# The first batch of a two-layer graph network: another order for its convolution

## The chip, the cores and the metric

The kernel runs on one core of one Trainium2 chip. The metric is the device time of one execution in microseconds (us). TensorE is called PE (its weight loads PEld), VectorE DVE, ScalarE ACT, GpSimd POOL and SyncE SP. Each engine works through its own queue in the order written; here that order is fixed by the program and not by a scheduler.

## The reference

There are 64 graphs of 256 nodes with 256 channels, all in float32. For this change, layer 0 matters:

```python
xc = transpose(x)                                    # channels first
h = relu(bn(conv1d(xc, conv1_w)))                    # "conv1": 1 tap
h = bn(conv1d(h, conv2_w, pad=8))                    # 17 taps along the nodes
x_conv = transpose(relu(h + xc))
s = x @ w_se.T + b_se                                # 3 numbers for each node
A = exp(-squared distances of s) * adj
msg = relu(x @ w_msg.T + b_msg)
x_nmp = A @ msg
# GRU gates: r, z = sigmoid(...), n = tanh(...) of [x_conv, x_nmp] and x
x = layernorm(x + (1 - z) * n + z * x)
# layer 1: layernorm, aggregation over adj, two projections, relu, layernorm
```

## The kernel before

The graphs go in eight batches of eight. The 17-tap convolution is not done tap by tap. The nodes of a graph are 16 positions (`j`) in 16 tiles (`t`); an exact polynomial transform over the positions (a tree of small rotations on DVE) turns the convolution into 16 "leaf" products with transformed filters on PE, three real products for each complex leaf. An inverse tree on DVE follows. The transformed filters have to be made once, in the first batch, from the weights; later batches read them back from DRAM (`w2m`).

In the main loop (one step for each graph) the gates and the second layer of a graph alternate on PE with pieces of the next batch's convolution; `pump()` hands out the pieces. Ahead of the loop the convolution of batch 0 has to be done alone, beside the making of the filters. That stretch is what the change touches:

```python
def filters(pool):            # 74 blocks of 7 output channels, in 20 groups of (mostly) 4
    ...                       # wt: 6 pieces of w2T, two buffers, fetched as buffers come free
    for i, (piece, starts) in enumerate(groups):
        WS[i + 2] = scaled(...)                    # DVE: ws = wt * scale of bn2
        TT[i + 1] = turned(WS[i + 1], ...)         # PE: 4 transposes; ACT: copy to tT
        for a, o in enumerate(starts):
            nc.tensor.matmul(ps, TT[i][:, a, :], tap_sb)      # PE: the taps' transform
            nc.scalar.copy(W2[0][:, c, :, ...], ps)           # ACT: into w2all
        # ... after the last group of an input half: six stores of w2all to w2m (6 MB)
        yield

def conv(b):
    # ... fetch(0), fetch(2): x of two graphs each
    yield None
    for g in range(0, BG, 2):                      # four pairs of graphs
        xTc = conv_pool.tile([P, C, 2 * N], F32, tag="xTc", bufs=1)
        # PE: 8 transposes of x; ACT: 2 copies into xTc; store of xTc to DRAM (xt); fetch(g + 4)
        for o in range(C):
            # PE: conv1, 2 matmuls of 512 columns
            # ACT: relu and batch norm into HP, 2 activations of 256
            yield PE_WEIGHT * 1.7
    yield None
    for j, r in ((0, 8), (8, 0)):                  # the fold: 4 operations of 2048 elements
        for first, op in ((V + r, ALU.subtract), (U + r, ALU.add)):
            nc.vector.tensor_tensor(...)
    yield from split_all(*TREES[0], S)             # DVE: the tree of V
    yield from butterflies([(S, V, V + 8, 8, True)])
    if b == 0: yield from split_u()                # DVE: the trees of U
    STAGE[b] = "products"
    # 8 items: products (PE), then take() (ACT copy, two DVE operations),
    # then merge steps (DVE), queued and handed out between the items
    STAGE[b] = "inverse"
    # second level: 8 operations of 512; third level: 8 operations of 512  (DVE)
    for q in range(4):
        xb = x_by_tiles(b, q)                      # 512 KB of x
        nc.vector.tensor_add(sl(V + 4 * q, 4), sl(V + 4 * q, 4), xb)
        # ... then 8 transposes (PE) and 4 relu activations (ACT) into xcs

# the first batch
fl = filters(first_pool)
# ... constants loaded: wms, rows, whh, wrr ...
for i in range(n_groups):                          # 20
    next(fl)
    while total < FRONT * (i + 1) / n_groups and 0 not in STAGE:
        total += next(first) or 0.0                # pieces of conv(0), conv1 among them
# ... conv(0) up to "inverse"; first_pool (w2all and the filters' buffers) closed
wih = weight(wihT, 2 * D, 3 * D, "wih", nc.sync, work)
for k in range(3):
    load(k)                                        # xT and adj of graph k
load_x(0)
early = [messages(0), messages(1), factors(0), distances(0), mask(0), factors(1),
         distances(1), mask(1), passing(0), messages(2)]
# ... one of them after every 1.5 units of conv(0)'s rest; then the main loop
```

`sl(a, n)` is `n` slots of the tile `XF`, 256 elements each; `stt` is DVE's scalar_tensor_tensor.

Of the kernel before, what the change touches and what calls it, by code (L numbers as in the profile page):

```python
# [12 lines left out]
F32 = mybir.dt.float32  # L13
# [3 lines left out]
P = 128  # L17
# [28 lines left out]
FRONT = 66.0  # L46
# [29 lines left out]
def gnn_two_layers(  # L76
# [38 lines left out]
    def x_by_tiles(b, q):  # L115

        t = conv_pool.tile([P, 4, D], F32, tag="xb", name="xb")
        nc.sync.dma_start(
            out=t, in_=x[b * BG:(b + 1) * BG].rearrange("g (t j) d -> (g t) j d", j=M)[:, 4 * q:4 * q + 4, :])
        return t  # L120
# [8 lines left out]
    tap_sb = const.tile([TAPS * OB, NM * OB], F32)  # L129
    nc.scalar.dma_start(out=tap_sb, in_=tb_dram.ap())  # L130
# [24 lines left out]
    def along_rows(pool):  # L155

        for i, v in enumerate((bn_scale[1], bn_shift[1])):
            ps = bank("ps_row")
            for c in range(C):
                dg = pool.tile([P, P], F32, tag="dg", name="dg", bufs=4)  # L160
                nc.vector.tensor_scalar(dg, ident, v[:, c:c + 1], None, ALU.mult)
                nc.tensor.matmul(ps[:, c * P:(c + 1) * P], ones, dg, start=True, stop=True)
            nc.scalar.copy(bn2_row[:, i, :], ps[:, :D])
# [3 lines left out]
    W2 = {}  # L167

    def filters(pool):
        W2[0] = pool.tile([P, C, NM, D], F32, name="w2all")  # L170
# [37 lines left out]
        along_rows(pool)  # L208
        TT = {}
        WS = {0: scaled(*groups[0]), 1: scaled(*groups[1])}  # L210
        TT[0] = turned(WS[0], 4)
        for i, (piece, starts) in enumerate(groups):
# [7 lines left out]
            for a, o in enumerate(starts):  # L220
                ps = bank("ps_w")
                nc.tensor.matmul(ps[:, :NM * OB], TT[i][:, a, :], tap_sb, start=True, stop=True)
                skip = OB - D % OB if o == D - OB else 0
                pv = ps[:, :NM * OB].rearrange("p (f o) -> p f o", o=OB)
                nc.scalar.copy(W2[0][:, c, :, o + skip:o + OB], pv[:, :, skip:])
            if i + 1 == len(groups) or pieces[groups[i + 1][0]][0] != c:
                for f in range(0, NM, 8):
                    g = min(f + 8, NM)
                    nc.sync.dma_start(out=w2m[f:g, c].rearrange("f p o -> p f o"), in_=W2[0][:, c, f:g, :])
# [60 lines left out]
    def merge(re, im, size, phis, scales, tmp, new):  # L290


        h, n = size // 2, len(phis)
        t_re, t_im = tmp, tmp + n * h
        same = all(abs(x0 - x1) < 1e-12 for s0, s1 in scales for x0, x1 in zip(s0, s1))
        for base, t in ((re, t_re), (im, t_im)):
            a, b = halves(base, n, size, False), halves(base, n, size, True)
            tt = temps(t, n, h)
            if same:
                nc.vector.tensor_sub(tt, a, b)  # L300
                yield cost(n * h)
                nc.vector.tensor_add(a, a, b)
                yield cost(n * h)
                continue

            assert n == 1 and h % 2 == 0
            for j in range(2):
                rho = scales[0][1][j] / scales[0][0][j]
                a2, b2 = sl(base + j, h // 2, 2), sl(base + h + j, h // 2, 2)
                stt(sl(t + j, h // 2, 2), b2, -rho, a2)  # L310
                yield cost(h // 2)
                stt(a2, b2, rho, a2)
                yield cost(h // 2)
        for k, phi in enumerate(phis):
            tan, c, turned = quarter(phi / 2)
            hr, hi = sl(re + k * size + h, h), sl(im + k * size + h, h)
            dr, di = sl(t_re + k * h, h), sl(t_im + k * h, h)
            if turned:
                stt(hr, dr, -tan, di)
                yield cost(h)  # L320
                stt(hi, di, -tan, dr, op1=ALU.subtract)
            else:
                stt(hr, di, tan, dr)
                yield cost(h)
                stt(hi, dr, -tan, di)
            yield cost(h)
            new.append(scales[k][0] + [c * s for s in scales[k][0]])
# [16 lines left out]
    def merges(which, p, tmp, scales):  # L344
# [4 lines left out]
        while True:  # L349
            below = ([1.0], [1.0]) if s == 2 else (scales[s // 2, 2 * n], scales[s // 2, 2 * n + 1])  # L350
            new = []
            yield from merge(re + n * s, im + n * s, s, [levels[-(s.bit_length() - 1)][n]], [below], tmp + n * s, new)
            scales[s, n] = new[0]
            if s == size or n % 2 == 0:
                return
            n, s = n // 2, 2 * s
# [65 lines left out]

    def conv(b):
# [14 lines left out]
        for g in range(0, BG, 2):  # L438
# [12 lines left out]
            for o in range(C):  # L451
# [7 lines left out]
                yield PE_WEIGHT * 1.7  # L459
        yield None  # L460
        for j, r in ((0, 8), (8, 0)):
            hv = HP[:, j:j + 8].rearrange("p j c g k -> p (j c g) k")
            for first, op in ((V + r, ALU.subtract), (U + r, ALU.add)):
                nc.vector.tensor_tensor(sl(first, 8).rearrange("p s (r t) -> p (s r) t", t=M),  # L464
                                        hv[:, :, 0:M], hv[:, :, 1:M + 1], op)
                yield cost(8)
# [9 lines left out]
        for _ in range(4):  # L476
            yield None
        sv, s8, s4 = {}, {}, {}
        todo = [(lambda k=k: products(b, 2 * k, S + 2 * k), merges(0, k, S, sv)) for k in range(4)]
        todo += [(lambda k=k: products(b, 8 + 2 * k, S2 + 2 * k), merges(1, k, S2, s8)) for k in range(2)]  # L480
        todo += [(lambda: products(b, 12, S2 + 4), merges(2, 0, S2 + 4, s4)), (lambda: last_products(b), None)]
        vector = deque([other])
        share, spent = (39.0 if b == 0 else 61.0) / len(todo), 0.0
        beyond = 1.0 - 0.85 * 5.2 / (share + 2 * cost(2))
        for i, (make, after) in enumerate(todo):
# [14 lines left out]
            if after:  # L500
# [12 lines left out]
        for j in range(4):  # L513
# [4 lines left out]
        for j in range(8):  # L518
            stt(sl(V + j, 2, 8), sl(V + j, 2, 8), sv[j], sl(U + j, 2, 8))
            yield cost(2)  # L520

        xcs = [work.tile([P, C, 4, N], F32, tag="xc", name="xc", bufs=3) for _ in range(2)]

# [13 lines left out]
        for q in range(4):  # L537
            xb = x_by_tiles(b, q)
# [9 lines left out]
        for g in range(BG):  # L548
            XC[b * BG + g] = (xcs[g // 4], g % 4)
# [4 lines left out]
    def load(k):  # L554
# [3 lines left out]
        XT[k] = work.tile([P, C, N], F32, tag="xT", name="xT", bufs=4)  # L558
        nc.sync.dma_start(out=XT[k], in_=xt_dram[k // 2][:, :, (k % 2) * N:(k % 2 + 1) * N])
        ADJ[k] = work.tile([P, C, N], F32, tag="adj", name="adj", bufs=5)  # L560
# [7 lines left out]
    def messages(k):  # L568
        MSG[k] = work.tile([P, C, D], F32, tag="msg", name="msg", bufs=3)
        st = sts[k % len(sts)]  # L570
        twice = st.rearrange("p m (r e) -> p m r e", e=SR)
        for m in range(C):
            ps = bank("ps_msg")
            for c in range(C):
                nc.tensor.matmul(ps[:, :D + 4], XT[k][:, c, m * P:(m + 1) * P], wms[:, c, :],  # L575
                                 start=(c == 0), stop=(c == C - 1))
            nc.vector.tensor_add(twice[:, m, :, 0:3], ps[:, D:D + 3].unsqueeze(1).to_broadcast([P, 2, 3]),
                                 bse_row.unsqueeze(1).to_broadcast([P, 2, 3]))
            nc.vector.tensor_add(MSG[k][:, m, :], ps[:, :D], bmsg)  # L579
        nc.scalar.activation(MSG[k], MSG[k], AF.Relu)  # L580

        sq = work.tile([P, C, 3], F32, tag="sq", name="sq")
        ns = work.tile([P, C], F32, tag="ns", name="ns", bufs=3)
# [7 lines left out]
    def factors(k):  # L591
# [4 lines left out]
        lr = work.tile([ROWS, 2, N], F32, tag="lr", name="lr", bufs=1)  # L596
# [4 lines left out]
    def distances(k):  # L601
        lr, ns = ST[k]
        AT[k] = work.tile([P, C, N], F32, tag="AT", name="AT")
# [146 lines left out]
    first, total = conv(0), 0.0  # L750
    with tc.tile_pool(name="first", bufs=1) as first_pool:
        fl = filters(first_pool)
# [3 lines left out]


# [15 lines left out]
        bse_row = const.tile([P, 3], F32)  # L773
        nc.sync.dma_start(out=bse_row, in_=bse.rearrange("r o -> o r").to_broadcast([P, 3]))
        bmsg = const.tile([P, D], F32)
        nc.sync.dma_start(out=bmsg, in_=rows[:, R_MSG:R_MSG + D].to_broadcast([P, D]))
# [6 lines left out]
        bhh = first_pool.tile([P, 2 * D], F32, name="bhh")  # L783
        nc.sync.dma_start(out=bhh, in_=rows[:, R_HH:R_HH + 2 * D].to_broadcast([P, 2 * D]))
# [8 lines left out]
        total += next(first)  # L793
        n_groups = 20
        for i in range(n_groups):
            next(fl)
            while total < FRONT * (i + 1) / n_groups and 0 not in STAGE:
                total += next(first) or 0.0
        for _ in fl:
            pass  # L800
        nc.vector.tensor_add(brzn[:, :2 * D], brzn[:, :2 * D], bhh)
        nc.gpsimd.tensor_scalar(wrr, wrr, 0.5, None, ALU.mult)
        nc.gpsimd.tensor_scalar(brel, brel, 0.5, None, ALU.mult)
        while STAGE.get(0) != "inverse":
            total += next(first) or 0.0

    work = ctx.enter_context(tc.tile_pool(name="work", bufs=2))
    wih = weight(wihT, 2 * D, 3 * D, "wih", nc.sync, work)
    for k in range(3):
        load(k)  # L810
    load_x(0)
    early = [lambda: messages(0), lambda: messages(1), lambda: factors(0), lambda: distances(0), lambda: mask(0),
# [118 lines left out]
```

## Time and profile before

The time is the median of three runs; the rest is from the profile of one execution, whose span is 2314.6 us.

| | |
|---|---|
| median (lowest to highest) | 2314.66 us (2311.76 to 2317.57) |
| PE busy | 2225.2 us (96%) |
| DVE busy | 1685.2 us (73%) |
| ACT busy | 766.0 us (33%) |
| POOL busy | 468.7 us (20%) |
| mean DMA rate | 98 GB/s |

A line of the timeline shows start and length in us, engine, line, operation, output and inputs with their shapes, count, and in brackets how long the engine had been idle and what ended that. The table by stages shows a window, its length and the busy time and instruction count of each engine. A float32 matmul is two records on PE, a transpose one. Busy time of PE is modelled, since matmuls are pipelined; a stage with PE always busy can still be one at a low clock, so the granted clock stands beside it.

### The profile page before, as it was taken

The numbers are of one execution on the slowest core, as the hardware profiler recorded it, in microseconds if no ns is written. First come the engines' busy times: TensorE is split into PE (matmuls) and PEld (weight loads), VectorE is DVE, ScalarE is ACT, GpSimd is POOL, SyncE is SP. The second block draws the span as 40 slices with busy tenths as digits, with TensorE's granted clock in tenths as the row PEclk, the third lists the DMA queues.
The fourth block names the chain that finished last, engine by engine and source line by source line (L and its number), as shares of the span: only waits on it lengthen the run. The fifth ranks groups of instructions, "written<-read, shape, count | busy, mean of one in ns | idle before, by whom it ended". The sixth has DMA issues, their size and how long they took to land.

```text
span 2314.6 us, 24215 instructions
## 1 busy us (share of the span) xinstructions
PE 2225.2 (96%) x8262; PEld 1456.2 (63%) x8262; DVE 1685.2 (73%) x3212; ACT 766.0 (33%) x1577; POOL 468.7 (20%) x925
## 2 busy tenths in 40 slices
PE   7879999999999999999999999999999999999996
PEld 4565566666666666666666566665666656666663
DVE  2893998759794788829887498956889398874543
ACT  4514222442224321353224332253223532243332
POOL 1000221312122222202212131221222122121211
PEclk8998999999999999999999999999999999999998
DMA  5543152224323144221532234222433214321100
GB/s 176 156 161 114 59 170 67 85 94 130 118 73 109 50 137 132 74 100 37 169 99 73 101 106 143 75 96 69 136 105 101 94 43 151 113 78 37 46 23 14
DMA packets 211128, 226.66 MB, mean 98 GB/s; under 512 B 22087, under 2 KB 201790, under 8 KB 211006
## 3 DMA queue, kind: packets, MB, share of 16 engines
q1 hardware_dynamic: 188448, 191.14, 26.2%
q10 hardware_dynamic: 22558, 33.99, 4.2%
q8 instruction: 66, 1.08, 0.2%
q14 instruction: 56, 0.46, 0.1%
HBM read 179.22 MB, written 45.88 MB: 97 GB/s over the span
## 4 chain that ended last, share of the span: by engine, by line
PE 69%; DVE 21%; DMA 4%; issue 3%; POOL 2%; ACT 1%; ACTq 0%; SPq 0%; DVEq 0%; POOLq 0%
PE ps_rz L637 14%; PE ps_k L383 12%; DVE XF L103 8%; PE ps_n L649 7%; PE ps_rz L635 7%; PE ps_out L712 6%; PE ps_c L454 5%; PE ps_nmp L619 4%; PE ps_n L647 4%; PE ps_out L724 3%; PE ps_msg L575 3%; DVE w L103 2%; DVE XF L464 2%; DVE bst L654 2%; DMA w<-w2m 2%
## 5 line engine op out<-in xcount | busy, mean ns | idle before, releaser
L103 DVE SCALAR_TENSOR_TENSOR XF<-XF 128x512 f32<-128x512 f32 (+2 forms) x800 | 506.7, 664 | 7.0
L676 POOL TENSOR_SCALAR q<-mv 128x2 f32<-128x2 f32 x64 | 32.1, 502 | 1459.1 <-DVE mv L655 1459.1
L383 PE MATMUL ps_k<-w,XF 128*128 128x256 f32 x1316 | 302.1, 385 | 15.2 <-ACT AT L609 11.6
L383 PEld LDWEIGHTS ps_k<-w,XF 128*128 128x128 f32 x1316 | 248.5, 192 | 64.1 <-ACT AT L609 17.3
L650 DVE TENSOR_TENSOR gn<-ps_n,brzn 128x512 f32<-128x512 f32 x128 | 88.1, 688 | 239.4 <-PE ps_n L649 239.4
L641 ACT ACTIVATE rz<-rz 128x512 f32<-128x512 f32 x128 | 80.7, 631 | 509.9 <-DVE rz L640 509.9
L635 PE MATMUL ps_rz<-whh,xT 128*128 128x512 f32 x512 | 240.8, 592 | 0.0
L637 PE MATMUL ps_rz<-wih,xc 128*128 128x512 f32 x512 | 240.6, 592 | 0.0
L637 PE MATMUL ps_rz<-wih,nmp 128*128 128x512 f32 x512 | 240.6, 592 | 0.0
L712 PE MATMUL ps_out<-wrr,hT 128*128 128x512 f32 x512 | 232.8, 598 | 5.5 <-ACT hT L701 5.5
L640 DVE TENSOR_TENSOR rz<-ps_rz,brzn 128x512 f32<-128x512 f32 x128 | 87.2, 681 | 192.2 <-PE ps_rz L637 192.2
L637 PEld LDWEIGHTS ps_rz<-wih,nmp 128*128 128x128 f32 x512 | 97.3, 190 | 122.5 <-issue 122.5
L637 PEld LDWEIGHTS ps_rz<-wih,xc 128*128 128x128 f32 x512 | 97.2, 190 | 122.5 <-issue 121.5
L712 PEld LDWEIGHTS ps_out<-wrr,hT 128*128 128x128 f32 x512 | 98.1, 192 | 105.2 <-issue 89.6
L580 ACT ACTIVATE msg<-msg 128x512 f32<-128x512 f32 x64 | 40.4, 631 | 353.1 <-DVE msg L579 353.1
L575 PE MATMUL ps_msg<-wms,xT 128*128 128x260 f32 x512 | 134.1, 402 | 12.5 <-DMA adj<-in_adjT_dram 8.1
L635 PEld LDWEIGHTS ps_rz<-whh,xT 128*128 128x128 f32 x512 | 92.2, 190 | 64.5 <-issue 61.2
L647 PE MATMUL ps_n<-whh,xT 128*128 128x256 f32 x512 | 131.6, 379 | 0.0
L649 PE MATMUL ps_n<-wih,xc 128*128 128x256 f32 x512 | 131.4, 379 | 0.0
L649 PE MATMUL ps_n<-wih,nmp 128*128 128x256 f32 x512 | 131.4, 379 | 0.0
L360 DVE TENSOR_TENSOR XF<-XF 128x512 f32<-128x512 f32 (+3 forms) x128 | 125.2, 1004 | 1.8
L454 PE MATMUL ps_c<-xTc,w 128*128 128x512 f32 x256 | 118.1, 604 | 7.6 <-ACT xTc L446 7.6
(105 smaller groups left out, 3486.6 us busy)
## 6 DMA issues: line engine op xcount, KB each, us to landing
w<-w2m SPq DMA_DIRECT2D x105, 768.0 KB, 5.9
xn<-in_x_dram SPq DMA_DIRECT2D x32, 512.0 KB, 4.3
xt<-xTc ACTq DMA_DIRECT2D x32, 512.0 KB, 3.3
xT<-xt SPq DMA_DIRECT2D x64, 256.0 KB, 3.0
adj<-in_adjT_dram SPq DMA_DIRECT2D x64, 256.0 KB, 2.8
x<-in_x_dram SPq DMA_DIRECT2D x64, 256.0 KB, 3.1
xb<-in_x_dram SPq DMA_DIRECT2D x32, 512.0 KB, 4.9
out_dram<-y ACTq DMA_DIRECT2D x64, 256.0 KB, 2.2
```

Of the source, the lines that this page charges most:

```text
L103: nc.vector.scalar_tensor_tensor(o, in0, s, in1, op0=op0, op1=op1)
L360: (nc.vector.tensor_add if add else nc.vector.tensor_sub)(sl(o, n), sl(a, n), sl(b, n))
L383: nc.tensor.matmul(ps, X[:, slot, c * P:(c + 1) * P], w(m, c), start=(c == 0), stop=(c == C - 1))
L454: nc.tensor.matmul(ps, w1[:, c, o * P:(o + 1) * P], xTc[:, c, :], start=(c == 0), stop=(c == C - 1))
L575: nc.tensor.matmul(ps[:, :D + 4], XT[k][:, c, m * P:(m + 1) * P], wms[:, c, :], start=(c == 0), stop=(c == C - 1))
L619: nc.tensor.matmul(ps[:, d * N:(d + 1) * N], MSG[k][:, m, d * P:(d + 1) * P], AT[k][:, m, :], start=(m == 0), stop=(m == C - 1))
L635: nc.tensor.matmul(prz, XT[k][:, c, q], whh[:, c, 0:2 * D], start=(c == 0), stop=False)
L637: nc.tensor.matmul(prz, t, wih[:, i, 0:2 * D], start=False, stop=(i == 3))
L647: nc.tensor.matmul(pn[:, D:], XT[k][:, c, q], whh[:, c, 2 * D:], start=(c == 0), stop=(c == C - 1))
L649: nc.tensor.matmul(pn[:, :D], t, wih[:, i, 2 * D:], start=(i == 0), stop=(i == 3))
L650: nc.vector.tensor_add(RZ[k][1][:, n, :], pn, brzn[:, 2 * D:])
L712: nc.tensor.matmul(ps, hT[:, c, n * P:(n + 1) * P], wrr[:, c, :], start=(c == 0), stop=(c == C - 1))
```

## The change

Only the first batch is changed. conv1 of all four pairs now goes first, without filter work in between, and each pair is folded on DVE as soon as it is there. Then the filters are made, with the transform of the folded data beside them. The messages and distances of the first graphs, which before came after the leaf products, stand between them; their tiles (`ahead`) lie in space that is free once the filters are made, so that they need not wait for `w2all`. Messages of the first graphs use ACT in place of DVE (the bias comes in by a product with a row of ones). The outputs are made by quarters: x is no longer added on DVE, but on PE by products with the identity, into the same bank as the result. Merges of the first batch do both halves of a complex value in one operation.

```diff
@@ conv1 first, then the filters
-        total += next(first)
-        n_groups = 20
-        for i in range(n_groups):
-            next(fl)
-            while total < FRONT * (i + 1) / n_groups and 0 not in STAGE:
-                total += next(first) or 0.0
+        next(first)
+        along_rows(filter_pool, 1, bn2_row)
+        next(fl)
+        places = 0
+        for t in first:
+            places += t is None
+            if places == 5:
+                break
+        def filter_steps(last):
+            nonlocal done, groups
+            while groups < last:
+                next(fl)
+                groups += 1
+                while done < 40.0 * groups / 19 and 0 not in STAGE:
+                    done += next(first) or 0.0
+        filter_steps(15)
         ... (loads of the constants; before, they stood ahead of all this)
+        store_w2(0)                # before: after the last group of this half
+        filter_steps(20)
@@ the fold by pairs (in the loop over the pairs)
+            if b == 0:
+                yield from fold(g, g + 2)
         yield None
-        for j, r in ((0, 8), (8, 0)):
-            ...
+        if b > 0:
+            yield from fold(0, BG)
@@ messages between the leaf products
+    ahead = ctx.enter_context(tc.tile_pool(name="ahead", bufs=1, side="right"))
+    for k in range(3):
+        load_xt(k)
+    FIRST["xb"] = [x_by_tiles(0, slice(q, M, 4), "xb" if q < 2 else "xTc") for q in range(3)]
+    store_w2(1)
+    early = deque([lambda: messages(0, True), lambda: messages(1, True), lambda: factors(0),
+                   lambda: messages(2, True), lambda: distances(0), lambda: factors(1), lambda: distances(1)])
+    while STAGE.get(0) != "inverse":
+        if next(first) == PE_WEIGHT and early:
+            early.popleft()()
+    first_pool.close()
     work = ctx.enter_context(tc.tile_pool(name="work", bufs=2))
+    for k in range(3):
+        load_adj(k)
     wih = weight(wihT, 2 * D, 3 * D, "wih", nc.sync, work)
@@ messages(k, idle)
+            if idle:
+                nc.tensor.matmul(ps[:, :D + 4], ones[0:1, :], bms[0:1, :], start=False, stop=True)
+                nc.scalar.copy(twice[:, m, :, 0:3], ps[:, D:D + 3].unsqueeze(1).to_broadcast([P, 2, 3]))
+                nc.scalar.activation(MSG[k][:, m, :], ps[:, :D], AF.Relu)
+                continue
@@ outputs by quarters (batch 0)
+            def turned_x(q):
+                ...
+                        nc.tensor.matmul(pss[o][:, j * P:(j + 1) * P], xb[:, j, o * P:(o + 1) * P], ident,
+                                         start=(j == 0), stop=False)
+            held = [turned_x(0), turned_x(1)]
+            for q in range(4):
+                yield from second(q)
+                yield from third(q)
+                yield from third(q + 4)
+                pss = held.pop(0)
+                ... (8 products of X[:, V + q + 4 * j] with ident, into the same banks, stop=(j == 3))
+                ... (4 relu activations into xcs)
+                if q < 2:
+                    held.append(turned_x(q + 2))
+                yield None
@@ merges (batch 0: joint)
+        both = X[:, re:re + 2 * (im - re)].rearrange("p (b s) e -> p b s e", b=2)
+            for v in (slice(0, 2),) if joint else (0, 1):
+                nc.vector.tensor_sub(tt[:, v], a[:, v], b[:, v])
+                nc.vector.tensor_add(a[:, v], a[:, v], b[:, v])
@@ the main loop
-            while done < total * at / goal:
+            while done < CONV_WEIGHT * at / goal:      # 107.7, in place of the sum counted in batch 0
```

In batch 0 each item's merges now follow its take directly, and the four pauses ahead of the products are left out there.

## The prediction

> **What bounds the kernel now.** I read the stage table first (busy time in windows that I cut where the kind of work changes), then the timelines of PE and DVE in the first 190 us, then the waits, and last the instruction orders of the two kernels. The columns of the first view are the window, its length, busy us and instruction count of PE, PEld, DVE, ACT and POOL, then granted clock, DMA share and GB/s.
>
> ```profile
> 0.00:45.60 45.60, 32.66 (x106) 19.74 (x107) 4.68 (x20) 19.27 (x38) 6.67 (x15) 0.89 0.69 208
> 45.60:110.40 64.80, 51.57 (x191) 34.21 (x190) 60.17 (x79) 38.04 (x83) 0.00 (x0) 0.89 0.44 130
> 110.40:151.40 41.00, 40.93 (x189) 35.40 (x187) 36.50 (x69) 4.86 (x11) 0.00 (x0) 1.00 0.46 151
> 151.40:190.20 38.80, 20.68 (x77) 14.98 (x78) 34.09 (x67) 10.30 (x23) 7.15 (x17) 0.69 0.53 175
> 190.20:2314.60 2124.40, 2079.41 (x7706) 1351.89 (x7704) 1549.79 (x2981) 693.52 (x1426) 454.88 (x893) 0.99 0.29 92
> ```
>
> The first gate product starts at 190.2 us. From there PE is busy 2079.4 of 2124.4 us: that loop is PE's, and nothing in it is shortened. The change can only move the 190.2. Ahead of it the limit changes by stage. Until 45.6 DVE has done 4.7 us: it waits for the whole conv1, which is interleaved with the first three filter groups. From 45.6 to 110.4 DVE is busy 60.2 of 64.8 us and PE follows it. To 151.4 PE is full with the leaf products. Then DVE again, with PE waiting at a low clock (0.69).
>
> ```profile
> 45.59 2.29 DVE L464 TENSOR_TENSOR XF<-XF 128x2048 f32<-128x2048 f32 x1 [29.70 <-ACT XF L457]
> 96.20 0.66 DVE L191 TENSOR_TENSOR ws<-wt,bn_row 128x476 f32<-128x476 f32 x1 [3.80 <-DMA wt<-in_w2T_dram]
> ```
>
> DVE's first fold sat 29.7 us behind conv1; later a load of filters kept it 3.8 us. PE in the filter stage, when it is fed and when it is not:
>
> ```profile
> 53.56 1.18 PE L200 MATMUL ps_tT<-ident,ws 128*119 128x128 f32 x4 [2.09 <-DVE ws L191]
> 54.53 3.55 PE L222 MATMUL ps_w<-tap_sb,tT 119*128 119x329 f32 x8
> 57.91 0.60 PE L200 MATMUL ps_tT<-ident,ws 128*119 128x128 f32 x4
> 58.35 2.38 PE L222 MATMUL ps_w<-tap_sb,tT 119*128 119x329 f32 x8
> 60.57 0.60 PE L200 MATMUL ps_tT<-ident,ws 128*119 128x128 f32 x4
> ```
>
> A fed group of four blocks takes 60.57 - 57.91 = 2.66 us; behind a wait of 2 us the same work takes from 53.56 to 57.91, 4.35 us. PE's waits up to 191 us, largest first:
>
> ```profile
> PE ps_tT L200 <- DVE ws L191: 15.9, 10, 2.6
> PE ps_msg L575 <- DMA adj<-in_adjT_dram: 8.1, 1, 8.1
> ```
>
> The second is the gap after the leaf products: the space of the filters must be free before the loads of the loop may start.
>
> **What the Trainium skill says.** "TensorE: Matmul & The Clock Gate", section "What's actually happening", has the array at half rate after an idle window of about 3.4 us and at full rate after as long a busy one. The trace agrees in kind: 3.55 against 2.38 us for the same eight records. "VectorE: DVE Perf Modes", section "The TRN2 errata — SBUF-src ops pay a fixed extra latency per instruction", gives an fp32 tensor_tensor as (N+151)/0.96 ns: 2291 ns for 2048 elements; the fold shows 2.29. So joining two short operations saves only the fixed part. "DMA: Bandwidth & Descriptors", section "Issuing engines are not separate DMA queues", says that all queues share 16 engines; so the order on the sync queue decides what the filters' loads collide with. The trace agrees: the load that kept DVE at 96.2 was issued at 83.6 behind 6 MB of filter stores and took 12.5 us.
>
> **The change, stage by stage.** All PE work of the 190 us stays and some is added; only its order and its neighbours change.
>
> *conv1 alone.* The first transposes end at 5.13 + 1.94 = 7.1, the four row products at 9.4 (as before). conv1 of the first pair then takes PE to about 13.3, and its last eviction ends at 14.3. A later pair is a cycle: first copy 0.6, conv1 3.7, eviction of the second half 1.0, as at 21.50 to 26.91 before: 5.4. Three cycles: 30.5 us instead of 46. The single transpose buffer must also be stored before it is filled again; at 22.6 that took 7.0 us, but with 2.5 MB of constants in flight, which now come later. I take it as hidden. The folds become sixteen of 512 elements, (512+151)/0.96 = 0.69 us each or some 0.62 apart; twelve hide in conv1, four remain: 33.0.
>
> *Filters.* Seventy-four blocks are 18.5 full groups of 2.66 = 49.2 us of PE. ACT, at 58.61, 61.26 and 64.02 for its groups, needs 2.7 too. DVE in this stage has 16 scalings of 0.57, two of 0.2, and of the transform six stt of 1024 at 1.15, four of 512 at 0.62, four two-row ones at 1.17, eight of 256 at 0.37, eight two-row ones at 0.63, three butterflies of 2.2 and small ones of 6.2: 43 us, so DVE could be through at 33 + 43 = 76. PE starts at 31 and sets the end: 80.5 if nothing slips. The first three groups still go at DVE's pace (0.57 + 2.3 = 2.9), and three engines at 2.4 to 2.7 us per group leave no slack: plus 3, so 83.5 against 110.4. This is the largest gain, 27 us. The filter stores no longer stand among the filter loads.
>
> *Leaf products with messages.* PE: 188 records of 40.98 us as before; three messages of 1.9 + 0.9 us (the bias becomes a one-row product) are 8.3; transposes and distances 1.7. Together 51 us, to 134.5. DVE: with the two halves joined a small merge takes 0.72 + 0.62 + 0.75 = 2.1 us instead of 2.4, a take 1.25, the next size 3.6, the largest 7.3. After the fourth product, taken at about 114 because three messages lie ahead, remain (1.25+2.1+3.6+7.3) + (1.25+2.1) + (1.25+2.1+3.6) + (1.25+2.1) + 1.0 = 29 us: 143. DVE, not PE, ends this stage, and PE stops for a PSUM bank near its end. The added 10 us of PE are thus mostly free. The messages' loads need only the filters' working space, free at 83.5; 256 KB in 3 to 4 us lands before the first message at 88.7.
>
> *Tail.* From 143: butterflies 2.0, combinations 2.5, a mask 0.7, first quarter four operations of 0.63 = 2.5: 150.7. The four additions of x (4 x 1.22) leave DVE and become products with the identity; so do the transposes. Such a product is two records where a transpose is one: 16 transposes take 2.06 us, hence 0.25 for one product and 2.0 for eight. PE behind the first quarter has 4 x 2.0 of results, 2 x 2.0 of x, and 1.8 of message passing = 13.8, and starts cold after seven idle us, where the first 4 us do half the work: about +1. First gate at 165.5. Loads for it (masks first, then the input weights) are issued when the last leaf product has read the filters, near 139, and have 8 us to the mask and 26 to the gates.
>
> *Sum.* 165.5 against 190.2: 24.7 us less. The first stages gain 27, the products and their tail take 82 instead of 80, since messages and identity products have to be done in them. In the loop the PE order of the two kernels is the same instruction for instruction; on DVE one 256-element butterfly per batch moves, and the fixed pacing constant changes nothing in that order. I give it 0 +- 2. 2314.7 - 24.7 = 2290.
>
> **Rivals.**
> *Balanced as meant:* DVE does not lag behind the products, PE ends them at 134 and the tail is 20 us. For it: before, DVE did 36.5 us in 41 us of products. Against it: the largest merge stands ahead of the fifth take in a strict order. First gate near 156: 2280.
> *Coupling eats the filter stage:* scaling, turning, copying, product, copying are a chain over three engines with two or three buffers, and a PE that waits 1 us in each group drops to the low clock (0.89 here). With 3.3 us a group the stage ends at 95: 2302. Against it: DVE has less per group than before, where 60.2 us of work lay in it.
> *The transpose buffer:* if its store takes 7 us in each cycle, conv1 ends 5 us later: 2295.
> *A new wait on the first messages:* the stores of the first half of the filters (6 MB; at the 340 GB/s that the transfers of the kernel before reach in their fullest stretches, 18 us) are ahead of these loads on the queue. If they start after 68 us, the first message stalls PE and the second product behind it: up to 8 us, 2298.
> *Exposed loads in the tail:* before, 8.1 us were lost there; were the masks late again, 2295.
>
> **Range and chances.** The first is 10 below, the others 5 to 12 above, and they rarely come together; 2281 to 2299 should hold it in eight of ten. Faster by 2% would need 46 us, a first gate at 144: the lead-in and PE's work alone, 9 + 14 + 49 + 51 + 14 = 137, leave 7 us for every wait. Slower by 2% would need a fault in the loop. Chances 0.03, 0.96, 0.01.
>
> **What would show it right or wrong.** Right: the last fold before 35 us; the scalings no longer PE's largest wait; filter groups 2.7 apart; the first leaf product at 81 to 87; DVE without gaps from the fourth take on; PE idle some 7 us ahead of the first quarter; the first gate at 160 to 171; from there 2122 to 2126 us. Wrong: the first gate earlier because the takes are on time, or later through a wait on the xT or adj loads; or the loop itself longer or shorter than 2124 by more than 3 us.

## The result and the profile after

The changed kernel takes 2302.14 us (four runs, 2301.71 to 2302.88) against 2315.36 us for the kernel before beside it (2311.76 to 2317.57): a ratio of 0.9945, 95% interval 0.9928 to 0.9962. That is a gain of 13.2 us, where 25 had been expected. The profiled execution has a span of 2300.6 us.

The table by stages of the kernel after, cut at the last fold, the first leaf product, the end of the leaf products and the first gate product. Its columns are the window, its length, busy us and count of PE, PEld, DVE, ACT and POOL, the granted clock, the DMA share and GB/s:

```profile
0.00:30.45 30.45, 23.02 (x80) 13.34 (x80) 11.12 (x29) 13.79 (x26) 3.04 (x13) 1.00 0.68 200
30.45:80.70 50.25, 49.38 (x217) 34.85 (x216) 49.77 (x73) 42.83 (x94) 3.84 (x2) 1.00 0.59 166
80.70:145.30 64.60, 58.75 (x237) 45.13 (x236) 42.41 (x66) 10.23 (x30) 3.11 (x15) 0.89 0.54 183
145.30:178.28 32.98, 19.69 (x138) 18.89 (x137) 26.40 (x42) 7.52 (x16) 2.44 (x3) 0.74 0.50 159
178.28:2300.60 2122.32, 2079.39 (x7706) 1352.68 (x7704) 1549.13 (x2981) 692.03 (x1422) 452.30 (x893) 0.99 0.29 92
```

From the first gate product on nothing has moved: 2122.3 us with the same 7706 records on PE (2124.4 before). The first two rows are all that was wanted of them: both PE and DVE are full from 30.45 to 80.70, at full clock. The loss is in the third row: 64.6 us where PE has 58.75 us of work at a clock of 0.89, and DVE has 22 us without work. PE's timeline through both stages:

```profile
59.23 0.60 PE L203 MATMUL ps_tT<-ident,ws 128*119 128x128 f32 x4
...
61.89 0.60 PE L203 MATMUL ps_tT<-ident,ws 128*119 128x128 f32 x4
...
80.71 5.58 PE L380 MATMUL ps_k<-w2all,XF 128*128 128x256 f32 x24
92.15 2.07 PE L626 MATMUL ps_msg<-wms,xT 128*128 128x260 f32 x4 [5.85 <-DMA w2m<-w2all]
94.15 1.23 PE L629 MATMUL ps_msg<-bms,ones 1*128 1x260 f32 x2
95.31 2.10 PE L626 MATMUL ps_msg<-wms,xT 128*128 128x260 f32 x4
...
98.51 7.83 PE L380 MATMUL ps_k<-w2all,XF 128*128 128x256 f32 x24
106.18 1.04 PE L626 MATMUL ps_msg<-wms,xT 128*128 128x260 f32 x4
```

The filter groups run 2.66 us apart (61.89 - 59.23) without a wait. Then the first message waits 5.85 us, and what follows is slow: four records of a message take 2.07 us here and 1.04 us at 106.18; the second leaf product takes 7.83 us where the first, with as many records, took 5.58. The windows of PE over that stretch show that this is the clock, in the third column from the end:

```profile
92.00:94.00 2.00, 1.85 (x4) 1.17 (x4) 0.00 (x0) 0.00 (x0) 0.00 (x0) 0.50 0.92 271
...
100.00:102.00 2.00, 2.00 (x6) 1.63 (x5) 1.93 (x4) 0.00 (x0) 0.22 (x1) 0.50 1.09 387
102.00:104.00 2.00, 2.00 (x7) 1.59 (x6) 1.07 (x3) 0.00 (x0) 0.00 (x0) 0.66 1.09 386
104.00:106.00 2.00, 2.00 (x11) 1.75 (x10) 0.00 (x0) 0.00 (x0) 0.00 (x0) 1.00 1.09 385
```

The reason for the wait is in the sync queue's timeline (start, length of the issuing, queue, line, transfer, count):

```profile
67.86 15.44 SPq L171 DMA_DIRECT2D w2m<-w2all  x6
83.41 5.81 SPq L607 DMA_DIRECT2D xT<-xt  x3
```

Six filter stores of 1 MB (the last of 896 KB) stand ahead of the messages' xT loads, and issuing them alone takes 15.4 us. The wait is put down to a store, but the semaphore events of the trace show the load: the last store landed at 91.15 us, the first xT load (issued at 83.4) at 91.84, and PE's next instruction came 0.1 us after that.

DVE's timeline shows what this costs further down. Its takes come in the order of the products, and all stand behind that gap:

```profile
99.57 0.69 DVE L396 TENSOR_TENSOR XF<-XF,ps_k 128x512 f32<-128x512 f32 x1 [10.45 <-ACT XF L395]
...
110.55 0.69 DVE L396 TENSOR_TENSOR XF<-XF,ps_k 128x512 f32<-128x512 f32 x1 [7.44 <-ACT XF L395]
...
124.54 0.69 DVE L396 TENSOR_TENSOR XF<-XF,ps_k 128x512 f32<-128x512 f32 x1 [3.17 <-ACT XF L395]
...
154.26 0.42 DVE L417 TENSOR_TENSOR XF<-ps_k,bn_row 128x256 f32<-128x256 f32 x1
```

The line at 124.54 is the fourth take. After it DVE never waits until the last operation of the products at 154.26, so whatever delays the fourth take delays the first gate product. Each take begins with a copy on ACT, and in ACT's order that copy stands behind the evictions of the message in front of it. The first product was finished at 86.3 us; its copy came at 98.95, directly behind the first message:

```profile
98.67 0.39 ACT L631 ACTIVATE msg<-ps_msg 128x256 f32<-128x256 f32 x1
98.95 0.59 ACT L395 COPY XF<-ps_k 128x512 f32<-128x512 f32 x1
```

PE's waits to 178 us (sum, times, longest) then hold what is left of the old ones:

```profile
PE ps_xc L554 <- DVE XF L103: 10.5, 1, 10.5
PE ps_msg L626 <- DMA w2m<-w2all: 5.9, 1, 5.9
```

The wait for the scalings (15.9 us in ten pieces before) is gone, and so is the one for adj (8.1 us). The 10.5 us are PE waiting for DVE ahead of the first quarter.

### The profile page after: what moved, and what is told of

It reads as the page before. It is cut to its first block, busy times and chain, and to the rows that moved or that the text cites. A ratio compares the mean times of both kernels' runs of the same rounds, so it can differ in the third digit from the quotient of the medians.

```text
span 2300.6 us, 24425 instructions
## 1 busy us (share of the span) xinstructions
PE 2230.2 (97%) x8370; PEld 1464.9 (64%) x8370; DVE 1678.8 (73%) x3188; ACT 766.4 (33%) x1585; POOL 464.7 (20%) x926
## 4 chain that ended last, share of the span: by engine, by line
PE 74%; DVE 19%; issue 2%; DMA 1%; POOL 1%; ACT 1%; SPq 1%; ACTq 0%; POOLq 0%; DVEq 0%
PE ps_rz L694 16%; PE ps_k L380 11%; PE ps_n L706 8%; PE ps_rz L692 8%; DVE XF L103 7%; PE ps_out L769 6%; PE ps_c L461 5%; PE ps_nmp L676 4%; PE ps_n L704 4%; PE ps_msg L626 4%; PE ps_out L781 3%; DVE w L103 2%; DVE bst L711 1%; DVE XF L427 1%; PE ps_xc L574 1%
## 5 line engine op out<-in xcount | busy, mean ns | idle before, releaser
L380 PE MATMUL ps_k<-w,XF 128*128 128x256 f32 x1316 | 301.8, 385 | 13.3 <-ACT AT L666 11.6
L770 ACT COPY hr<-ps_out 128x256 f32<-128x256 f32 x128 | 47.6, 372 | 232.6 <-PE ps_out L769 232.6
```

The costliest lines, as they stand in the source:

```text
L380: nc.tensor.matmul(ps, X[:, slot, c * P:(c + 1) * P], w(m, c), start=(c == 0), stop=(c == C - 1))
```

## Experiments

The theories. *Load:* the xT loads behind the stores stop PE, and the low clock after it doubles the harm; together some 11 us. *Clock alone:* a part of that is only the clock, and would go if PE were kept busy through the wait. *Position:* the messages would cost even with their data there, because they stand ahead of the fourth take in a strict order and DVE has no slack after it. Rivals: the DMA traffic itself slows PE or DVE, or the joined merges and the tail were mis-sized. For the stage that went well there is a question of its own: which part of the change brought it. Every first gate product named below is that of one execution. The first leaf product, before which PE and DVE have the same order in the changed kernel and the first six runs, came between 80.09 and 82.14 us in them; so a difference of 2 us or less is put down to an edit only when it is still there counted from the first leaf product.

### The xT loads ahead of the filter stores

```diff
-    store_w2(0)                    # six stores, before filter_steps(20)
     filter_steps(20)
     ... (xT and xb loads)
+    store_w2(0)
     store_w2(1)
```

> The only edit: the loads of xT and of x by quarters stand ahead of both halves of the filter stores on the sync queue. Theory 1 (the first messages waited 5.9 us for xT behind 6 MB of stores, and the low clock after that wait cost about as much again): no wait ahead of the first message, messages and second product at full rate, so the second product ends at about 95 us instead of 106.3; DVE's chain behind the fourth product moves by the same amount, first gate at about 167, time 2302 - 11 = 2291. Theory 2 (DVE's chain of takes and merges sets the end whatever PE does before): first gate moves by less than 3 us, time above 2299.

Measured: 2292.75 us, ratio to before 0.9891 (0.9874 to 0.9908); span 2289.8. Timeline of PE in this run:

```profile
80.92 5.58 PE L380 MATMUL ps_k<-w2all,XF 128*128 128x256 f32 x24
86.34 1.04 PE L626 MATMUL ps_msg<-wms,xT 128*128 128x260 f32 x4
...
89.64 5.45 PE L380 MATMUL ps_k<-w2all,XF 128*128 128x256 f32 x24
```

No wait, the short durations, and the second product ends at 95 in place of 106. The three loads landed 2.9 to 4.2 us after their issue. The first gate product comes at 167.23 us in place of 178.28: 11.05 us, the whole of *load*. From 92 to 110 us the transfers (filter stores among them) moved 364 to 386 GB/s, with PE always busy at full clock beside them, so traffic as such is not the cause.

### The wait kept, but PE kept busy in it

```diff
+    def warm():                    # products whose result nobody reads, ahead of messages(0)
+        ps = bank("ps_warm")
+        for _ in range(7):
+            nc.tensor.matmul(ps, ident, W2[0][:, 0, 0:2, :]..., start=True, stop=True)
```

> Seven products of 512 columns into an unused bank (6.0 us of PE at full rate) between the first leaf product and the first message, in the time in which PE waits; nothing reads them. Theory 1a (half of the loss is the clock): the wait shrinks to nothing on the record, the first message still starts at about 92.2, but it and the second product take 8.6 us instead of 14.0, first gate at about 173, time about 2297. Theory 1b (the loss is all in the wait, and the long durations are the loads' contention, not the clock): messages and product stay at 14 us, time 2302.

Measured: 2295.86 us, ratio 0.9907 (0.9892 to 0.9922); first gate product at 172.83 us. PE's timeline of this run, and its window of that stretch:

```profile
86.71 6.17 PE L889 MATMUL ps_warm<-w2all,ident 128*128 128x512 f32 x14
92.72 1.10 PE L626 MATMUL ps_msg<-wms,xT 128*128 128x260 f32 x4
```

```profile
92.00:98.00 6.00, 6.00 (x24) 3.70 (x23) 0.84 (x2) 1.48 (x5) 1.05 (x5) 1.00 1.01 300
```

The first message starts no earlier than in the changed kernel (92.72 against 92.15), yet the first gate product is 5.45 us earlier. So the 11.05 us are about half waiting and half clock: useless work gained five microseconds, only by keeping the clock.

### The messages from the fourth item on

```diff
-        if next(first) == PE_WEIGHT and early:
-            early.popleft()()
+        if next(first) == PE_WEIGHT:
+            item += 1
+            for _ in range({4: 1, 5: 1, 6: 2, 7: 2, 8: 1}.get(item, 0)):
+                early.popleft()()
```

> The loads stay as in the changed kernel; the messages, factors and distances come behind the fourth leaf product and later, not behind the first. If the position of the messages in PE's order is what delays the fourth take: four products without a gap from 80.7 to 102, fourth take at about 105 instead of 123.9, the 29 us chain of DVE ends near 137 instead of 154, first gate at about 160, time about 2284. If DVE's own work from 87 us on is the bound: the end of the takes moves by less than 10 us, time above 2292.

Measured: 2282.58 us, ratio 0.9848 (0.9832 to 0.9865); first gate product at 158.28 us. The loads have time here too, so this run is to be held against the one with the loads first: 167.23 - 158.28 = 9.0 us, of which 0.8 lie ahead of the first leaf product (80.09 against 80.92), so that 8.1 are due to position. PE's line for the leaf products of this run:

```profile
80.09 21.12 PE L380 MATMUL ps_k<-w2all,XF 128*128 128x256 f32 x96
```

Four products run through, and the first three takes come at DVE's own pace. The fourth does not. Its product is finished at 101.2 us, but on ACT its copy stands behind the evictions of the first message, and DVE waits:

```profile
104.52 0.39 ACT L631 ACTIVATE msg<-ps_msg 128x256 f32<-128x256 f32 x1
104.80 0.59 ACT L395 COPY XF<-ps_k 128x512 f32<-128x512 f32 x1
```

```profile
105.42 0.69 DVE L396 TENSOR_TENSOR XF<-XF,ps_k 128x512 f32<-128x512 f32 x1 [2.64 <-ACT XF L395]
```

So *position* has two parts, PE's order and ACT's. With the loads first, DVE waited 1.24, 5.06 and 3.17 us ahead of the first, second and fourth take; here 2.64 are left, and those come from ACT's order alone. Messages in their old place on PE, with the take's copy ahead of them on ACT, were not tried.

### The messages after all leaf products

```diff
     while STAGE.get(0) != "inverse":
-        if next(first) == PE_WEIGHT and early:
-            early.popleft()()
+        next(first)
+    while early:
+        early.popleft()()
```

> All messages, factors and distances of the first graphs behind the last leaf product, where PE waits 13 us for DVE in the changed kernel; loads as there. PE ends the leaf products at about 123 (held up a little by banks), the messages lie in 123 to 134, DVE ends its takes and merges near 132 instead of 154, first gate at about 156, time about 2280. Against it: if the distances come too late for the first mask (ready after 135), some 3 us more.

Measured: 2281.24 us, ratio 0.9844 (0.9829 to 0.9859); first gate product at 155.40 us. PE's timeline, and two windows of the same run:

```profile
81.16 40.98 PE L380 MATMUL ps_k<-w2all,XF 128*128 128x256 f32 x188
121.98 1.04 PE L626 MATMUL ps_msg<-wms,xT 128*128 128x260 f32 x4
...
135.92 6.65 PE L541 MATMUL ps_xc<-ident,xb 128*128 128x128 f32 x32
142.47 2.43 PE L554 MATMUL ps_xc<-ident,XF 128*128 128x128 f32 x16
```

```profile
81.20:122.00 40.80, 40.80 (x190) 35.62 (x189) 39.70 (x63) 4.83 (x10) 0.00 (x0) 1.00 0.83 285
122.00:142.50 20.50, 18.76 (x82) 13.20 (x80) 19.92 (x33) 6.36 (x21) 7.58 (x17) 0.83 0.49 160
```

DVE is busy 39.70 of 40.80 and 19.92 of 20.50 us: it sets this stretch alone. The messages lie in time that PE had to wait anyway, in the place of the 10.5 us gap; the x products after them even run mostly at half clock (6.65 us for 32 records, where 16 take 1.95 later), at no cost: the product behind them starts at 142.47, directly behind the DVE operation that it needs, which ends at 142.42. Against the run with the loads first that is 11.8 us. *Position* holds, and is as large as *load*.

### The x products still further ahead

```diff
# on top of the run before
-            held = [turned_x(0), turned_x(1)]
+            held = [turned_x(0), turned_x(1), turned_x(2)]
+            yield None
-                if q < 2:
-                    held.append(turned_x(q + 2))
+                if q < 1:
+                    held.append(turned_x(q + 3))
```

> On the kernel with all messages behind the leaf products (first gate at 155.4, time 2281): three quarters of x instead of two and the message passing of the first graph stand ahead of the first quarter's results in PE's order, in time in which PE waits for DVE. If PE's order sets the tail (13 us of PE behind the first quarter, ready at 142.4): what is left there is 5 times 1.95 us and the last quarter's wait for DVE, first gate at about 153, time about 2279. If DVE's quarters, 2.6 us apart, set it alone: first gate within 1 us of 155.4.

Measured: 2277.73 us (2277.26 to 2282.28), ratio 0.9837 (0.9819 to 0.9856). First gate product at 155.20, hardly earlier, because the first leaf product was 1.0 us later in this run; from one to the other it took 73.1 in place of 74.2 us. So 1.1 us of the expected 2: the x products, now 48 records, start at the low clock and take 7.70 us, so that with the message passing behind them PE comes to the first quarter at 146.27, when DVE has had it ready since 143.99. In time it cannot be told from the run before. The lowest median of the study is this version's, and it beats both kernels of the case.

### The merges as two halves again

```diff
# on top of "after all leaf products"
-  merges(0, k, S, sv, b == 0)      # and the two other calls
+  merges(0, k, S, sv, False)
```

> On the kernel with all messages behind the leaf products: merges of the first batch do real and imaginary half in operations of their own, as before the change. DVE has no gap there from the first take on, so each microsecond of its work should be seen: 7 small merges of 0.3 us more and 3 of 0.25 more, first gate 2.9 us later at 158.3, time about 2284. Rival: joining saves only what overlaps anyway, first gate within 0.7 us of 155.4.

Measured: 2281.24 us, ratio 0.985 (0.9826 to 0.9874); first gate product at 155.38 us, 74.7 us after the first leaf product in place of 74.2: no difference in time, as the rival said. DVE goes from its first take to the last product's in 44.2 us (88.96 to 133.20) in place of 43.2 (89.73 to 132.96). DVE's timeline of one small merge, first joined (the run before), then in halves (this run):

```profile
91.05 0.69 DVE L298 TENSOR_TENSOR XF<-XF 128x512 f32<-128x512 f32 x1
91.77 0.69 DVE L300 TENSOR_TENSOR XF<-XF 128x512 f32<-128x512 f32 x1
92.50 0.76 DVE L103 SCALAR_TENSOR_TENSOR XF<-XF 128x256 f32<-128x256 f32 x2
```

```profile
90.27 0.43 DVE L298 TENSOR_TENSOR XF<-XF 128x256 f32<-128x256 f32 x1
90.73 0.43 DVE L300 TENSOR_TENSOR XF<-XF 128x256 f32<-128x256 f32 x1
91.08 0.42 DVE L298 TENSOR_TENSOR XF<-XF 128x256 f32<-128x256 f32 x1
91.53 0.42 DVE L300 TENSOR_TENSOR XF<-XF 128x256 f32<-128x256 f32 x1
91.87 0.75 DVE L103 SCALAR_TENSOR_TENSOR XF<-XF 128x256 f32<-128x256 f32 x2
```

Joined, the two operations start 0.72 and 0.73 us apart; in halves, four starts are 0.46, 0.35, 0.45 and 0.34 apart. Where the next operation works on other data (sum of one half, difference of the other) its start comes 0.11 us sooner, ahead of the end of the one before. So 0.14 us is saved in a small merge (2.13 us to the next take against 2.27), not a fixed part for each operation left out.

### conv1 among the filters again, and the stores among them

```diff
# on top of "after all leaf products"; first run: conv1 handed out between the filter groups
-        for t in first:                          # no more conv1 ahead of the filters
-            places += t is None
-            if places == 5: break
-                while done < 40.0 * groups / 19 and 0 not in STAGE:
+                while done < 66.0 * groups / 20 and 0 not in STAGE:
# second run: the first half's stores where they become possible
-        filter_steps(15)
+        filter_steps(10)
+        store_w2(0)
+        filter_steps(15)
         ... (loads of the constants)
-        store_w2(0)
# third run: both
```

First run:

> On the kernel with all messages behind the leaf products: conv1 is again handed out among the first filter groups at the pace of the kernel before (66 units over 20 groups), while stores and constants keep their new places and the fold stays by pairs. If conv1 first is what brings the filters' end from 110 to 81 (it gives DVE its transform early): first leaf product at 100 to 105, first gate at about 174, time about 2300. If moving the loads and stores off the filters' loads did it: first leaf product before 88, first gate before 163, time below 2289.

Measured: 2294.21 us, ratio 0.9906 (0.9887 to 0.9925); first leaf product at 96.53 us, first gate product at 169.71. It lies between the two expectations.

Second run:

> On the kernel with all messages behind the leaf products: only the stores of the first filter half go back to their old place on the sync queue, ahead of the last load of filter weights. If such a store holds up that load as in the kernel before (12.5 us to landing): DVE and PE wait for it in the filter stage, first leaf product at about 92, first gate at about 165, time about 2290. Rival: two buffers hide it, first leaf product within 2 us of 81.

Measured: 2291.95 us, ratio 0.9895 (0.9878 to 0.9913); first leaf product at 96.92 us. Timelines of the sync queue and of DVE:

```profile
58.76 11.63 SPq L171 DMA_DIRECT2D w2m<-w2all  x6
70.49 3.23 SPq L187 DMA_DIRECT2D wt<-in_w2T_dram  x1
```

```profile
82.47 0.66 DVE L194 TENSOR_TENSOR ws<-wt,bn_row 128x476 f32<-128x476 f32 x1 [11.56 <-DMA wt<-in_w2T_dram]
```

The last piece of the filters' weights is issued at 70.49, behind the stores, and is there at 82.4: DVE stands for 11.56 us, and PE after it.

Third run:

> Both of the last two edits together: conv1 among the filter groups, and the stores of the first filter half ahead of the last load. Alone each moved the first leaf product from 81.2 to about 96.7 us. If the two losses are separate (one is DVE starting late, the other DVE waiting for a load): they add, first leaf product at about 112, as in the kernel before the change (110.4), time about 2307. If they overlap (DVE, late anyway, meets the load when it has landed): first leaf product at 98 to 103, time about 2296, and the rest of the 29 us comes from the loads of the constants and of x.

Measured: 2298.40 us (2297.53 to 2299.31), ratio 0.9931 (0.9909 to 0.9954). First leaf product at 103.15 us, first gate product at 176.30; PE's waits for the scalings in this run:

```profile
PE ps_tT L203 <- DVE ws L194: 17.4, 8, 5.1
```

Against 81.16 us each part alone costs 15.4 and 15.8 us at the first leaf product, both together 22.0 and not 31. They overlap: with conv1 among the filters the groups go so slowly that part of the load's delay lies behind them, and DVE stands for this load 5.10 us here, not 11.56. The 15.9 us of waits for the scalings before are here again as 17.4. Of the 29.2 us by which "after all leaf products" has its first leaf product earlier than the kernel before, these two parts together bring 22.0; the other 7.2 come from what these runs left as changed (the later constants and the fold by pairs among it) and were not taken apart.

## Why the prediction was off

The sum said 165.5 us for the first gate product and it came at 178.28, 12.8 us later; the loop, given as 0 +- 2, was 2.1 us shorter.

- *conv1 alone:* right. A cycle is 5.29 us (26.11 - 20.82 between two conv1 in PE's timeline; 5.4 said), the last fold ends at 33.0 (33.0 said). The transpose buffer's store stayed hidden.
- *Filters:* right for PE, and the 3 us set aside for slips were not needed: 80.7 against 83.5, so -2.8. For DVE it was wrong: the items listed add up to 44.4 us and not 43, and DVE was through with the transform at 89.1 us, not at 76. That cost nothing here, since PE set the end of the filters and the first take came at 99.57 anyway. With the messages behind all leaf products it shows: the first take (89.73) directly follows the transform, although its product was finished at 86.7 and ACT's copy at 85.7. The rival of a coupled filter stage did not come true. That 27 us came under one heading was fair: neither the order of conv1 nor the stores alone would have brought them.
- *Leaf products with messages:* here the prediction failed, at the step "256 KB in 3 to 4 us lands before the first message at 88.7". Such a load does take 2.9 to 4.2 us when it is first in the queue; behind 6 MB of stores the first took 8.4 us (83.4 to 91.84). The fourth take came 43.8 us after the first leaf product (124.54 - 80.7), not 30.5: +13.3. With the loads first it is 32.4 (113.29 - 80.92). So 11.5 of the 13.3 are this step (43.84 - 32.37). Most of the rest is the size of a message: 3.3 us each (86.34 to 89.64 in that run) and not 2.8. The prediction had it as a rival, "A new wait on the first messages", with its condition ("If they start after 68 us"; they started at 67.86) all but met, but gave it "up to 8 us" and left it out of the sum. It counted the wait and not the clock after it, which doubled it.
- *The DVE chain after the fourth take:* right. 30.1 us (124.54 to 154.68) against 29; the joined small merge takes the 2.1 us said. What it was credited with was too much: in halves the same merge takes 2.27 and not 2.4 us.
- *Tail:* 23.6 us (154.68 to 178.28) against 22.5. The cold start was counted and is there: 3.96 and then 2.51 us for sixteen records that take 1.95 later. That is 2.6 us in all; the sum has 1 for it, though "the first 4 us do half the work" makes 2.
- -2.8 + 13.3 + 1.1 + 1.1 = 12.7 of the 12.8 us.

"The added 10 us of PE are thus mostly free" was wrong in another way. It was true of PE's work and false of its place: two messages ahead of the fourth product on PE, and a third ahead of its copy on ACT, held up DVE, which had no slack behind the fourth take, and moving them behind gained 11.8 us more. The prediction worked out the lateness of the fourth take correctly and did not ask whether it had to be.

The rival "Balanced as meant" named 156 for the first gate product; that figure was reached (155.4) once the messages were out of the way, though not by its mechanism: DVE still ended the stage, at 134.0, twelve microseconds after the last leaf product.

## To carry to other kernels

A load that someone will soon wait for belongs ahead of stores that nobody waits for, in the order of the queue, also where the stores could have begun earlier: here that was worth 11 us at one place and 16 at another. Before work is put into another engine's stage as filler, ask which engine is without slack behind it: here three messages among its first four inputs cost 11.8 us, and behind its last input they were free. Look at the order of every engine on the way, since evictions on ACT held up DVE even where PE had run on. And a stall of PE is to be priced with the clock after it, here as much again as the stall.

## Not expected of the hardware

- The half clock after the 5.85 us stall lasted until 103.4 us, so that PE was busy under it for 11 us, from 92.15 on; in the tail, after a longer gap of 10.5 us, the same was over at 168.2, 5 us after the start at 163.31. "TensorE: Matmul & The Clock Gate", section "What's actually happening", names about 3.4 us of sustained activity: the tail is near that, the stretch of the messages is not. Why it took so long there wasn't tried. Both stretches of half clock (89.7 to 103.4 and 151.2 to 168.2) and one in the run with the messages after all leaf products (135.0 to 141.8) are whole multiples of 3.41 us long: four, five and two. In the last, PE's longest wait in the 13 us ahead of the fall was 1.36 us; what made the clock fall there stays open.
- Issuing is itself held up by what stands ahead: the three xT loads took 0.54 to 0.61 us each to issue when first, and 1.4 to 2.6 us behind the stores. "DMA: Bandwidth & Descriptors", section "Issuing engines are not separate DMA queues", calls the time on the sequencer to initiate a DMA usually small relative to the DMA itself; six stores held the sync queue for 15.4 us here.
- Joining two pairs of DVE operations into one pair of double size saved only 0.14 us, since operations of 256 elements on different data overlap by some 0.1 us (starts 0.34 us apart, 0.42 long) and those on the same data don't (0.46 apart).
